# How the head stacks of block 2's attention are made: loads from DRAM, or one-hot products on chip

## The chip, the cores and the metric

The kernel runs on one core of a Trainium2 chip. The core's engines work side by side, each through its own instructions in order: TensorE (PE; its weight loads are listed apart as PEld) multiplies matrices into the accumulators (PSUM), VectorE (DVE) and ScalarE (ACT) work on elements, GpSimd (POOL) helps with elementwise work and fills, and SyncE (SP) issues all DMAs of this kernel into one queue. Times are device microseconds of a whole execution. The kernel before took 1585.57 us as the median of three runs (1581.46 to 1586.45).

## What is computed

The program is a perceiver of four blocks. 256 tokens of width 256, for a batch of 2, attend to a context of 4096 tokens, then to themselves, then pass through a feed-forward with experts; each step is added to the tokens. The change is in the self-attention of block 2. It scores by distance: queries, keys and values are one projection `Q`.

```
Q = (x @ W_k.T).reshape(B, S, H, dk).transpose(0, 2, 1, 3)      # 16 heads of 16
sq_norm = jnp.sum(Q * Q, axis=-1, keepdims=True)
dot = jnp.einsum('bhsk,bhtk->bhst', Q, Q)
scores = -(sq_norm - 2.0 * dot + sq_norm.transpose(0, 1, 3, 2)) * inv_sqrt_dk
attn = jax.nn.softmax(scores, axis=-1)
context_q = jnp.einsum('bhst,bhtk->bhsk', attn, Q)
merged = jnp.einsum('hkd,hvd->hkv', Wq_h, Wv_h)                 # W_k and W_v by head
attn_out = jnp.einsum('bhsk,hkv->bhsv', context_q, merged) * inv_sqrt_dk
return attn_out.transpose(0, 2, 1, 3).reshape(B, S, D) @ W_o.T
```

All of it is in float32. The kernel computes a product of two float32 matrices as three products of a high and a low part of each (`split` makes the parts, `mm3` the products).

## The kernel before, in words

**Lanes.** `run` interleaves two lanes of work, whose tiles carry a letter in the profile: `a` holds self-attention and feed-forward (`af(n, b)` runs those of block n for batch b), `x` the cross attentions. While lane `x` runs the cross attention of block 2 for batch 1 (`xattn`), lane `a` does the self-attention and feed-forward of block 2 for batch 0, then the queries of block 3's cross attention (`x3_queries`). Block 3's cross attention (`l3_xattn`) is a generator. First it takes the maxima of the scores of some key tiles, its early max steps: a product on PE (L1369), a maximum over 512 or 1024 columns on DVE (L1373, L1375). Then it hands over for block 2's work on batch 1 (`af(2, 1)`), and then it runs its main loop: maxima, scores (L1396), exponentials (L1397), values (L573). Its key tiles `xk` and query tiles `xq` are filled by a memset (L1281) and by loads from DRAM (L1358).

**Order.** Nothing in the source fixes the order of the instructions of an engine. The framework schedules all engines from its own model of durations (`schedule_with_timeline_sim=True`). A change of one stage can therefore move others. DMAs go out in the order of SP's instructions, one queue for all.

**Block 2's attention before (`l2_attn`).** For one batch: normalise and transpose the tokens, project (`proj_t`), split into parts `qT`. One product contracts all 128 partitions: a head's 16 channels of keys, high, high and low, against queries, high, low and high, and 2 + 2 rows for the squared norms against ones. So each head needs a stack, in which its parts lie one below the other on the partitions. [...] So `stack_tile` zeroes four tiles of four heads (two of keys, two of queries) on POOL and loads their rows of ones from a filling in DRAM; `qT` is written to DRAM (`aa2q`, 512 KB); and for each of the four groups of four heads six loads of 64 KB (`stack`) and two of norms (`rows_from`) build the stacks. The norms are made by PE: the squares times a selection matrix (`sq`, L1184), split, written to DRAM (`aa2s`). Then the scores (`mh_scores`: L566, exponentials L567), the values (`mh_values`, L573), the normalisation by the sums (`mh_finish`), and two projections; the product of `W_k` and `W_v` by head is folded into `bd`.

**Block 3's way.** `l3_ffn_attn`, the attention of block 3's feed-forward, makes stacks on chip: `picks` builds a matrix of shifted identities once, and `pair_stacks` multiplies it with the parts of a projection (L1591), so that the sum of two products holds two heads, one in each half of the partitions, with their parts in place. Its tile of ones and zeros, `extra`, adds the rows of ones during the eviction from PSUM (L1595 to L1599). Its row of shifts goes through two transposes, a copy and a DMA from SBUF to SBUF (L1640, L1642, L518).

Of the kernel before, what the change touches and what calls it, by code (L numbers as in the profile page):

```python
# [18 lines left out]
F32 = mybir.dt.float32  # L19
# [9 lines left out]
P = 128  # L29
# [171 lines left out]
def _consts():  # L201
# [7 lines left out]

    half = np.arange(2)[None, :, None] * 8 + (p // HD)[:, None, None]  # L210
    sq = np.where(half == np.arange(HEADS)[None, None, :], -0.5, 0.0).astype(np.float32)
# [10 lines left out]
        ("extra", ((p % 64 >= 48) & (p % 64 < 50)).astype(np.float32)[:, None]),  # L222
# [4 lines left out]
        ("sq", sq.reshape(P, -1)),  # L227
# [62 lines left out]
class Lane:  # L290
# [237 lines left out]
    def stack_tile(self, pool, tag, n, ones=(), heads=GRP):  # L528


        x = self.t(pool, [P, heads, n], tag, F32R, bufs=1)
        self.nc.gpsimd.memset(x.bitcast(F32), 0.0)
        for at, k in ones:
            for j in range(0, heads, GRP):
                self.rows_from(x[:, j : j + GRP, :].rearrange("p j n -> p (j n)"), at, k, self.top.fill_d[:k, : GRP * n])
        return x

# [19 lines left out]

    def mh_scores(self, mp, keys, queries, scale, tie=lambda inst: None):


        nc = self.nc
        p = self.t(mp, [P, GRP, S], "p", bufs=self.p_bufs)
        for a in range(0, GRP, 2):
            ps = self.score()
            for j in range(2):
                tie(nc.tensor.matmul(ps[:, j, :], lhsT=keys(a + j), rhs=queries(a + j), start=True, stop=True))  # L566
            self.last_exp = nc.scalar.activation(p[:, a : a + 2, :], ps, AF.Exp, scale=scale)  # L567
        return p
# [64 lines left out]
class Perceiver:  # L633
# [51 lines left out]
    def xattn_mean(self, xp, n, b, queries):  # L685
# [77 lines left out]
        def exponents(i):  # L763
            u, q = divmod(i, 2)
            p, su = k.t(xp, [P, self.UN], "p", bufs=2), k.t(k.sm, [P, 1], f"su{q}", bufs=4)
# [329 lines left out]
    def along(self, fp, g):  # L1095
# [5 lines left out]
        row = k.t(fp, [8, S], "grow", bufs=1)  # L1101
# [59 lines left out]

    def l2_attn(self, b, x):
# [3 lines left out]
        with k.pool("a2", bufs=1) as ap:  # L1166
            xnT = k.transposed(k.layernorm(x, ap), ap, "xnT")
            sel = k.const(ap, "sq").rearrange("p (m h) -> p m h", m=2)
# [4 lines left out]
            ks = [k.stack_tile(ap, f"k{i}", S, [(k.ADD, 2)]) for i in range(2)]  # L1173
            qs = [k.stack_tile(ap, f"q{i}", S, [(k.ADD + 2, 2)]) for i in range(2)]
            qT = k.t2(ap, [P, 2, S], "qT")
            sq = k.t(ap, [P, 2, S], "o")
            ps = k.proj_t(wk, xnT, 0)
            nc.scalar.activation(sq, ps, AF.Square)
            k.split(qT, ps)
            q_d = k.dram([2, 2, P, S], f"a2q{b}")  # L1180
            k.to_dram(qT, q_d)
            ps = k.mm()
            for m in range(2):
                nc.tensor.matmul(ps[:HEADS, :S], lhsT=sel[:, m, :], rhs=sq[:, m, :], start=m == 0, stop=m == 1)  # L1184
            sqs = k.t2(ap, [HEADS, S], "sqs")
            k.split(sqs, ps[:HEADS, :S])
            sqd = k.dram([2, HEADS, S], f"a2s{b}")
            for i, part in enumerate((sqs.h, sqs.l)):
                nc.sync.dma_start(sqd[i], part.bitcast(F32))
# [3 lines left out]
            k.copy(v[:, :, :, :HD], k.proj(wk, xnT).rearrange("p t (h d) -> p t h d", d=HD))  # L1193
            bd = k.t(ap, [P, 2, P], "bd")
# [6 lines left out]
            bdp = k.t2(ap, [P, 2, P], "bdp")  # L1201
            k.split(bdp, bd)
            o = k.t(ap, [P, 2, D], "o")
            for g in range(4):
                k4, q4 = ks[g % 2], qs[g % 2]
                g4 = slice(GRP * g, GRP * g + GRP)
                k.stack(k4, q_d, g4, k.KEYS)
                k.stack(q4, q_d, g4, k.QUERIES)
                k.rows_from(q4, k.ADD, 2, sqd[:, g4, :])
                k.rows_from(k4, k.ADD + 2, 2, sqd[:, g4, :])  # L1210
                acc = k.mm()
                ps = [k.mh_scores(ap, lambda j: k4[:, j, t * P : (t + 1) * P], lambda j: q4[:, j, :], 0.5) for t in range(2)]
                for t in range(2):
                    k.mh_values(ps[t], lambda j: v[:, t, 4 * g + j, :], acc, t == 0, t == 1)
                k.mh_finish(g, acc, o)()
            oT = k.transposed(o, ap, "xnT")
            mT = k.t2(ap, [P, 2, S], "qT")
# [8 lines left out]
    def l2_ffn(self, b, x):  # L1226
# [4 lines left out]
        with k.pool("f2", bufs=2) as fp:  # L1231
            br = k.row("f2.br", fp)
            xf = k.t(fp, [P, 2, S], "xf", bufs=1)
            xnT = k.transposed(k.layernorm(x, fp), fp, "xnT", plain=xf)
# [64 lines left out]
    def masks(self):  # L1299

        k, nc = self.a, self.nc
        with k.pool("mask", bufs=1) as mp:
# [8 lines left out]
            fill = k.t(mp, [4, 2048], "fill")  # L1311
            nc.gpsimd.memset(fill, 1.0)
            nc.sync.dma_start(self.fill_d, fill)
# [253 lines left out]

    PICK, PICK_BLOCKS = {"kl": 0, "ql": 1, "kh": 9, "qh": 17}, 25

    def picks(self, k, pool):  # L1570


        nc = self.nc
        x = k.t(pool, [P, 4, self.PICK_BLOCKS, HD], "pick", F32R, bufs=1)
        nc.gpsimd.memset(x.bitcast(F32), 0.0)
        eye = self.eye.rearrange("p (i a d) -> p i a d", i=4, a=2)
        for at in (2, 9, 10, 17, 19):
            nc.vector.tensor_copy(x[:, :, at : at + 5 : 4, :], eye)
        return x.rearrange("p i a d -> p i (a d)")

    def pair_stacks(self, k, pick, dst, src, kind, extra=None):


        nc = self.nc
        for m in range(2):
            for i in range(0, 4, 2):
# [339 lines left out]
```

## Time and profile before

| | us |
|---|---|
| median of three runs (1581.46, 1585.57, 1586.45) | 1585.57 |
| the profiled execution | 1590.7 |
| its span, from the first to the last instruction | 1588.9 |
| PE busy | 1387.5 (87%) |
| DVE busy | 1106.4 (70%) |
| ACT busy | 891.8 (56%) |
| POOL busy | 534.7 (34%) |
| mean clock that was granted to PE | 0.916 of full |

The profiled execution is 5.1 us above the median, which is within what runs of the kernel differ by. Busy times are sums over a span with stages of different limits: which engine bounds the kernel must be read stage by stage. Two consecutive matmuls overlap, so a matmul's own duration (0.28 us for 256 columns) is longer than its share of a busy queue. Where the profile names what ended an idle time ("<-DMA ak<-aa2q"), it is the event that came last, here the load of the stack tile `ak` from the DRAM tile `aa2q`. Names carry the lane's letter in front (`aqT` is `qT` of lane a).

| block 2's self-attention | batch 0 | batch 1 |
|---|---|---|
| projection written to DRAM | 721.41 | 932.10 |
| squares times the selection matrix, on PE | 721.53 | 930.14 |
| first scores on PE | 731.7 | 942.21 |
| output added to the tokens (L1223) | 790.35 | 986.11 |

### The profile page before, as it was taken

The page shows a single profiled execution, that of the slowest core. Times are in us where ns is not written, and L with a number is a line of the kernel's source. Part 1 is how long each engine was busy: PE and PEld are TensorE (multiplying, and loading weights), DVE is VectorE, ACT ScalarE, POOL GpSimd, SP SyncE. Part 2 cuts the span into 40 slices and gives each one's busy share as a digit, 9 for nine tenths or more (in the row PEclk, how much of TensorE's full clock was granted, in tenths as well). Part 3 has the DMA queues.
Part 4 walks back from the last instruction along what each step waited for, and adds up shares of the span by engine and source line. Part 5 has one row for each costly group of instructions (what it writes and reads, how often), then busy time and mean ns, then how long its engine had stood idle before and what let it go on. Part 6 is the DMA issues. An engine that isn't in the chain of part 4 may idle for free.

```text
span 1588.9 us, 29546 instructions
## 1 busy us (share of the span) xinstructions
PE 1387.5 (87%) x11278; PEld 1126.0 (71%) x11278; DVE 1106.4 (70%) x1895; ACT 891.8 (56%) x1669; POOL 534.7 (34%) x395
## 2 busy tenths in 40 slices
PE   6899798978999998989973679979999999888498
PEld 6898688968899998988973245645555554774387
DVE  6999755455577787865663666759999980566764
ACT  5676455556866656745631016648888889233242
POOL 6655244444455454663354000120000000530441
PEclk9999899979999999999996558879999999996699
DMA  8753165564556575546454512456676741200471
GB/s 292 224 150 115 51 177 172 187 192 160 166 160 207 161 217 162 160 143 187 134 143 122 85 59 57 111 131 114 113 116 111 114 71 31 85 1 3 175 254 35
DMA packets 126628, 212.32 MB, mean 134 GB/s; under 512 B 14212, under 2 KB 90532, under 8 KB 122964
## 3 DMA queue, kind: packets, MB, share of 16 engines
q1 hardware_dynamic: 126488, 210.45, 48.7%
q8 instruction: 89, 1.46, 0.4%
q14 instruction: 51, 0.42, 0.1%
HBM read 181.72 MB, written 29.01 MB: 133 GB/s over the span
## 4 chain that ended last, share of the span: by engine, by line
PE 46%; DVE 16%; DMA 9%; ACT 4%; POOL 3%; issue 2%; SPq 1%; DVEq 0%; ACTq 0%; POOLq 0%
PE amm L405 9%; PE xacc L573 7%; DVE xpm L1375 6%; PE xmm L405 5%; PE xf L1369 5%; PE xs L405 4%; PE xpr L405 3%; DMA awr<-in_w 3%; PE amm L1396 2%; DMA xk<-akh_d 2%; PE xs L1396 2%; PE amm L1756 2%; PE xmm L777 1%; PE amm L573 1%; POOL aw L397 1%
## 5 line engine op out<-in xcount | busy, mean ns | idle before, releaser
L1375 DVE TENSOR_REDUCE xpm<-xf 128x2 f32<-128x1024 f32 x232 | 281.7, 1222 | 34.2 <-PE xf L1369 31.9
L397 POOL TENSOR_TENSOR aw<-awr,aw 128x1024 fp32r<-128x1024 f32 (+1 forms) x61 | 145.7, 2390 | 299.8 <-ACT aw L395 294.0
L1397 ACT ACTIVATE xp<-amm 128x512 f32<-128x512 f32 x299 | 170.1, 595 | 31.0 <-PE amm L1396 17.9
L395 ACT CAST aw<-awr 128x1024 fp32r<-128x1024 f32 (+1 forms) x114 | 115.5, 1016 | 116.0 <-DMA awr<-in_w 69.5
L405 PE MATMUL xmm<-xvx,xpT 128*128 128x256 f32 x1152 | 167.0, 291 | 4.5 <-DVE xpT L780 2.5
L573 PE MATMUL xacc<-xp,xv 128*17 128x256 f32 x2048 | 165.7, 397 | 0.9 <-DVE xot L591 0.9
L405 PE MATMUL xs<-xkx,xqkT 128*128 128x256 f32 x1152 | 164.0, 286 | 1.4 <-POOL xkx L727 0.6
L727 POOL TENSOR_TENSOR xvx<-xraw,xvx 128x512 fp32r<-128x512 f32 x96 | 131.6, 1387 | 82.9 <-ACT xvx L725 72.1
L405 PEld LDWEIGHTS xmm<-xvx,xpT 128*128 128x128 f32 x1152 | 147.7, 193 | 8.0 <-issue 3.7
L405 PEld LDWEIGHTS xs<-xkx,xqkT 128*128 128x128 f32 x1152 | 149.2, 193 | 3.5 <-POOL xkx L727 1.0
L1397 ACT ACTIVATE xp<-xs 128x512 f32<-128x512 f32 x213 | 123.5, 595 | 37.1 <-PE xs L1396 22.5
L1369 PE MATMUL xf<-xk,xq 49*128 49x512 f32 x464 | 125.4, 530 | 15.8 <-DVE xpm L1375 6.9
L1369 PEld LDWEIGHTS xf<-xk,xq 49*128 49x128 f32 x464 | 46.7, 195 | 114.4 <-issue 79.8
L399 DVE TENSOR_TENSOR aw<-awr,aw 128x1024 fp32r<-128x1024 f32 (+1 forms) x53 | 81.2, 1533 | 66.5 <-ACT aw L395 66.2
L405 PE MATMUL amm<-axnT,aw 128*128 128x256 f32 x648 | 101.1, 313 | 11.7 <-ACT axnT L395 6.9
L405 PEld LDWEIGHTS amm<-axnT,aw 128*128 128x128 f32 x648 | 92.3, 216 | 20.3 <-ACT axnT L395 9.7
L405 PE MATMUL amm<-ah,aw 128*128 128x256 f32 x768 | 99.3, 285 | 6.6 <-ACT au L1002 3.3
L1396 PE MATMUL amm<-xq,xk 51*128 51x256 f32 x598 | 99.6, 297 | 4.2 <-DVE aqT L393 2.9
L727 POOL TENSOR_TENSOR xkx<-xraw,xkx 128x512 fp32r<-128x512 f32 x48 | 72.3, 1506 | 89.8 <-ACT xkx L725 89.7
L405 PEld LDWEIGHTS amm<-ah,aw 128*128 128x128 f32 x768 | 94.3, 191 | 9.3 <-ACT au L1002 3.9
L1420 POOL TENSOR_TENSOR ax<-ax,ax 128x128 f32<-128x128 f32 x8 | 3.7, 458 | 281.8 <-DVE ax L603 281.8
L1396 PEld LDWEIGHTS amm<-xq,xk 51*128 51x128 f32 x598 | 83.9, 188 | 18.2 <-issue 12.6
(545 smaller groups left out, 2918.0 us busy)
## 6 DMA issues: line engine op xcount, KB each, us to landing
awr<-in_w SPq DMA_DIRECT2D x106, 512.0 KB
xraw<-in_ctxT SPq DMA_DIRECT2D x108, 256.0 KB
xraw<-in_ctx SPq DMA_DIRECT2D x96, 256.0 KB
xk<-akh_d SPq DMA_DIRECT2D x128, 128.0 KB
av_d<-xkvv SPq DMA_DIRECT2D x16, 544.0 KB
xv<-av_d SPq DMA_DIRECT2D x32, 272.0 KB
akh_d<-xkvk SPq DMA_DIRECT2D x32, 256.0 KB
akl_d<-xkvk SPq DMA_DIRECT2D x32, 256.0 KB
```

Source lines behind the costliest of these rows:

```text
L395: nc.scalar.copy(dst.h, src)
L397: lo.tensor_tensor(dst.l, src, dst.h.bitcast(F32), ALU.subtract)
L399: nc.vector.tensor_sub(dst.l, src, dst.h)
L405: tie(self.nc.tensor.matmul(out, lhsT=x, rhs=y, start=start and i == 0, stop=stop and i == 2))
L573: inst = self.nc.tensor.matmul(acc[STRIP * j : STRIP * j + v(j).shape[1], :S], lhsT=v(j), rhs=p[:, j, :], start=start, stop=stop)
L727: nc.gpsimd.tensor_tensor(x.l, r, x.h.bitcast(F32), ALU.subtract)
L777: tie(nc.tensor.transpose(pst[:, t * P : (t + 1) * P], p[:, t * P : (t + 1) * P], self.eye))
L1369: tie(nc.tensor.matmul(ps[h], lhsT=q4[rows, j, t * P : (t + 1) * P], rhs=k4[rows, j, :], start=True, stop=True))
L1375: nc.vector.tensor_reduce(at, both.rearrange("p (h n) -> p h n", h=2), axis=AX.X, op=ALU.max)
L1396: tie(nc.tensor.matmul(ps[h][:, j, :], lhsT=ks[c][rows, a + j, s * P : (s + 1) * P], rhs=q4[rows, a + j, :], start=True, stop=True))
L1397: exps = [nc.scalar.activation(p[:, h, a : a + 2, :], ps[h], AF.Exp, scale=0.25) for h in range(2)]
L1756: nc.tensor.matmul(ps[:, f, :], lhsT=w1[half][:, c, f * P : (f + 1) * P], rhs=buf[:, c, e * cap : (e + 1) * cap], start=c == 0, stop=c == 1)
```

## The change

Block 2's attention makes its stacks on chip, as block 3's does, for all 16 heads at once: 32 one-hot products and 8 evictions per batch, four of keys and four of queries. Two heads share a stack, in the lower and the upper 64 partitions, of which 52 rows are used. The one-hot matrix is built once ahead of block 2 and stays. `stack_tile`, the filling in DRAM, the write of `qT` and the loads of stacks are gone. The squared norms now come from the projection for the values, whose tokens lie on the partitions: Square on ACT, a sum over 16 columns on DVE, and a new function `pair_rows` that splits them, transposes them, copies the rows and sends them by eight DMAs into the stacks' norm rows. Block 3's attention uses `pair_rows` too. Tiles share places to make room: the layer normalisation uses the tile of `o` (or `u` in the feed-forward), `bd` that of `o`, `bdp` that of `qT`, the feed-forward's row of gates that of `xf`, and `xattn` keeps three buffers of row sums for four.

```diff
-        ("extra", ((p % 64 >= 48) & (p % 64 < 50)).astype(np.float32)[:, None]),
+        ("extra", np.stack([(p % 64 >= at) & (p % 64 < at + 2) for at in (3 * HD, 3 * HD + 2)], axis=1).astype(np.float32)),
...
-        ("sq", sq.reshape(P, -1)),
...
-            p, su = k.t(xp, [P, self.UN], "p", bufs=2), k.t(k.sm, [P, 1], f"su{q}", bufs=4)
+            p, su = k.t(xp, [P, self.UN], "p", bufs=2), k.t(k.sm, [P, 1], f"su{q}", bufs=3)
...
-        row = k.t(fp, [8, S], "grow", bufs=1)
+        row = k.t(fp, [8, S], "xf", bufs=1)
...
+    PICK, PICK_BLOCKS = {"kl": 0, "ql": 1, "kh": 9, "qh": 17}, 25
+    def picks(self, k, pool):
+        nc = self.nc
+        x = k.t(pool, [P, 4, self.PICK_BLOCKS, HD], "pick", F32R, bufs=1)
+        nc.gpsimd.memset(x.bitcast(F32), 0.0)
+        eye = self.eye.rearrange("p (i a d) -> p i a d", i=4, a=2)
+        for at in (2, 9, 10, 17, 19):
+            nc.vector.tensor_copy(x[:, :, at : at + 5 : 4, :], eye)
+        return x.rearrange("p i a d -> p i (a d)")
+    def pair_rows(self, k, pool, x, scale, dsts):
+        nc, n = self.nc, x.shape[3]
+        parts = k.t(pool, [P, 2, 2, 2, n], "pr_both", F32R, bufs=1)
+        nc.vector.tensor_scalar(parts[:, :, :, 0, :], x, scale, None, ALU.mult)
+        for t in range(2):
+            nc.vector.scalar_tensor_tensor(parts[:, t, :, 1, :], x[:, t], scale, parts[:, t, :, 0, :].bitcast(F32), ALU.mult, ALU.subtract)
+        ps = k.mm()
+        for t in range(2):
+            nc.tensor.transpose(ps[: 4 * n, t * P : (t + 1) * P], parts.bitcast(F32)[:, t].rearrange("p h a j -> p (h a j)"), self.eye)
+        rows = k.t(pool, [4 * n, S], "pr_row", F32R, bufs=1)
+        nc.vector.tensor_copy(rows, ps[: 4 * n, :S])
+        for dst, at in dsts:
+            for h in range(2):
+                k.rows_from(dst, h * self.HALF + at, 2, rows[2 * n * h : 2 * n * (h + 1)])
+    def pair_stacks(self, k, dst, src, kind, extra=None):
+        nc, pick = self.nc, self.pick
+        for m in range(2):
+            for i in range(0, 4, 2):
+                ps = k.mm2()
+                for j in range(2):
+                    for n, part in enumerate((src.h, src.l)):
+                        at = self.PICK[kind + "hl"[n]] * HD
+                        nc.tensor.matmul(ps[:, j, :], lhsT=pick[:, i + j, at : at + P], rhs=part[:, m, :], start=n == 0, stop=n == 1)
+                to = dst[:, 4 * m + i : 4 * m + i + 2, :]
+                k.flip ^= 1
+                if extra is None:
+                    nc.vector.tensor_copy(to, ps) if k.flip else nc.scalar.copy(to, ps)
+                elif k.flip:
+                    nc.vector.tensor_scalar(to, ps, extra, None, ALU.add)
+                else:
+                    nc.scalar.activation(to, ps, AF.Identity, bias=extra)
     def l2_attn(self, b, x):
         k, nc = self.a, self.nc
         wk, wv = k.weights("a2.wk", "a2.wv")
         (wo,) = k.weights("a2.wo")
         with k.pool("a2", bufs=1) as ap:
-            xnT = k.transposed(k.layernorm(x, ap), ap, "xnT")
-            sel = k.const(ap, "sq").rearrange("p (m h) -> p m h", m=2)
+            xnT = k.transposed(k.layernorm(x, ap, "o"), ap, "xnT")
             diag = k.const(ap, "diag")
             k.mh_tiles(ap)
-            ks = [k.stack_tile(ap, f"k{i}", S, [(k.ADD, 2)]) for i in range(2)]
-            qs = [k.stack_tile(ap, f"q{i}", S, [(k.ADD + 2, 2)]) for i in range(2)]
+            ks, qs = (k.t(ap, [P, HEADS // 2, S], tag, F32R) for tag in "kq")
             qT = k.t2(ap, [P, 2, S], "qT")
-            sq = k.t(ap, [P, 2, S], "o")
-            ps = k.proj_t(wk, xnT, 0)
-            nc.scalar.activation(sq, ps, AF.Square)
-            k.split(qT, ps)
-            q_d = k.dram([2, 2, P, S], f"a2q{b}")
-            k.to_dram(qT, q_d)
-            ps = k.mm()
-            for m in range(2):
-                nc.tensor.matmul(ps[:HEADS, :S], lhsT=sel[:, m, :], rhs=sq[:, m, :], start=m == 0, stop=m == 1)
-            sqs = k.t2(ap, [HEADS, S], "sqs")
-            k.split(sqs, ps[:HEADS, :S])
-            sqd = k.dram([2, HEADS, S], f"a2s{b}")
-            for i, part in enumerate((sqs.h, sqs.l)):
-                nc.sync.dma_start(sqd[i], part.bitcast(F32))
+            k.split(qT, k.proj_t(wk, xnT, 0))
+            for dst, kind in ((ks, "k"), (qs, "q")):
+                self.pair_stacks(k, dst, qT, kind, self.extra[:, kind == "q" :][:, :1])
             v = k.t(ap, [P, 2, HEADS, STRIP], "v")
             nc.gpsimd.memset(v, 0.0)
             nc.gpsimd.memset(v[:, :, :, HD], 1.0)
-            k.copy(v[:, :, :, :HD], k.proj(wk, xnT).rearrange("p t (h d) -> p t h d", d=HD))
-            bd = k.t(ap, [P, 2, P], "bd")
+            ps = k.proj(wk, xnT)
+            k.copy(v[:, :, :, :HD], ps.rearrange("p t (h d) -> p t h d", d=HD))
+            sq = k.t(ap, [P, 2, D], "o")
+            nc.scalar.activation(sq, ps, AF.Square)
+            sums = k.t(k.sm, [P, 2, HEADS], "sq_sum")
+            nc.vector.reduce_sum(sums, sq.rearrange("p t (h d) -> p t h d", d=HD), axis=AX.X)
+            self.pair_rows(k, ap, sums.rearrange("p t (a h) -> p t h a", h=2), -0.5, [(ks, k.ADD + 2), (qs, k.ADD)])
+            bd = k.t(ap, [P, 2, P], "o")
             ps = k.mm2()
             for c in range(2):
                 for d in range(2):
                     k.mm3(ps[:, c, :], wk[d][:, c * P : (c + 1) * P], wv[d], d == 0, d == 1)
             for c in range(2):
                 nc.vector.scalar_tensor_tensor(bd[:, c, :], ps[:, c, c * P : (c + 1) * P], 0.25, diag, ALU.mult, ALU.mult)
-            bdp = k.t2(ap, [P, 2, P], "bdp")
+            bdp = k.t2(ap, [P, 2, P], "qT")
             k.split(bdp, bd)
             o = k.t(ap, [P, 2, D], "o")
             for g in range(4):
-                k4, q4 = ks[g % 2], qs[g % 2]
-                g4 = slice(GRP * g, GRP * g + GRP)
-                k.stack(k4, q_d, g4, k.KEYS)
-                k.stack(q4, q_d, g4, k.QUERIES)
-                k.rows_from(q4, k.ADD, 2, sqd[:, g4, :])
-                k.rows_from(k4, k.ADD + 2, 2, sqd[:, g4, :])
-                acc = k.mm()
-                ps = [k.mh_scores(ap, lambda j: k4[:, j, t * P : (t + 1) * P], lambda j: q4[:, j, :], 0.5) for t in range(2)]
+                acc, ps = k.mm(), []
+                for t in range(2):
+                    p = k.t(ap, [P, 2, 2, S], "p", bufs=k.p_bufs)
+                    for h in range(2):
+                        r = slice(h * self.HALF, h * self.HALF + k.ADD + 4)
+                        both = k.score()
+                        for j in range(2):
+                            nc.tensor.matmul(both[:, j, :], lhsT=ks[r, 2 * g + j, t * P : (t + 1) * P], rhs=qs[r, 2 * g + j, :], start=True, stop=True)
+                        nc.scalar.activation(p[:, :, h, :], both, AF.Exp, scale=0.5)
+                    ps.append(p.rearrange("p a h n -> p (a h) n"))
                 for t in range(2):
                     k.mh_values(ps[t], lambda j: v[:, t, 4 * g + j, :], acc, t == 0, t == 1)
                 k.mh_finish(g, acc, o)()
             oT = k.transposed(o, ap, "xnT")
-            mT = k.t2(ap, [P, 2, S], "qT")
+            mT = k.t2(ap, [P, 2, S], "k")
             ps = k.mm2()
             for c in range(2):
                 k.mm3(ps[:, c, :], bdp[:, c, :], oT[:, c, :], True, True)
...
-            xnT = k.transposed(k.layernorm(x, fp), fp, "xnT", plain=xf)
+            xnT = k.transposed(k.layernorm(x, fp, "u", bufs=2), fp, "xnT", plain=xf)
...
-            fill = k.t(mp, [4, 2048], "fill")
-            nc.gpsimd.memset(fill, 1.0)
-            nc.sync.dma_start(self.fill_d, fill)
...
-                parts = k.t(k.sm, [P, 2, 2, 2, 4], "sh_both8", F32R)
-                nc.vector.tensor_copy(parts[:, :, :, 0, :], nm)
-                nc.vector.tensor_sub(parts[:, :, :, 1, :], nm, parts[:, :, :, 0, :].bitcast(F32))
-                ps = k.mm()
-                for t in range(2):
-                    nc.tensor.transpose(ps[:16, t * P : (t + 1) * P], parts.bitcast(F32)[:, t].rearrange("p h a j -> p (h a j)"), self.eye)
-                sh = k.t(ap, [16, S], "sh_row", F32R, bufs=2)
-                nc.vector.tensor_copy(sh, ps[:16, :S])
-                for h in range(2):
-                    k.rows_from(qs[:, at : at + 4, :], h * self.HALF + k.ADD, 2, sh[8 * h : 8 * h + 8])
+                self.pair_rows(k, ap, nm, 1.0, [(qs[:, at : at + 4, :], k.ADD)])
...
+        self.extra = a.const(self.fix, "extra")
...
+                            else:
+                                self.pick = self.picks(a, early.enter_context(a.pool("pick")))
```

More of the change, by code (lines that the diff above doesn't have):

```diff
@@ L208, in _consts @@
     first = np.broadcast_to(8.0 - np.arange(8, dtype=np.float32), (P, 8))
-    half = np.arange(2)[None, :, None] * 8 + (p // HD)[:, None, None]
-    sq = np.where(half == np.arange(HEADS)[None, None, :], -0.5, 0.0).astype(np.float32)
     freq = (1.0 / np.float32(10000.0) ** (np.arange(0, 64, 2, dtype=np.float32) / np.float32(64))).astype(np.float32)
@@ L526 @@
     KEYS, QUERIES = (0, 0, 1), (0, 1, 0)
[L528 to L536, printed above, removed]
     def shift_rows(self, mp, nm, qs, step=1):
@@ L556, in shift_rows @@
         return rest
[L558 to L568, printed above, removed]
     def mh_values(self, p, v, acc, start, stop, after=None, tie=lambda inst: None):
@@ L1565, in f3_tiles, with l3_ffn_attn @@
         return qs, ks, v
[L1568 to L1586, printed above, removed]
-                ps = k.mm2()
-                for j in range(2):
-                    for n, part in enumerate((src.h, src.l)):
-                        at = self.PICK[kind + "hl"[n]] * HD
-                        nc.tensor.matmul(ps[:, j, :], lhsT=pick[:, i + j, at : at + P], rhs=part[:, m, :], start=n == 0, stop=n == 1)
-                to = dst[:, 4 * m + i : 4 * m + i + 2, :]
-                k.flip ^= 1
-                if extra is None:
-                    nc.vector.tensor_copy(to, ps) if k.flip else nc.scalar.copy(to, ps)
-                elif k.flip:
-                    nc.vector.tensor_scalar(to, ps, extra, None, ALU.add)
-                else:
-                    nc.scalar.activation(to, ps, AF.Identity, bias=extra)
-    def l3_ffn_attn(self, k, b, x, w, rows, tiles, picks, out):
+    def l3_ffn_attn(self, k, b, x, w, rows, tiles, out):
         nc = self.nc
@@ L1611, in l3_ffn_attn @@
             hT = k.transposed(hn, ap, "hT", scale="f3.g1", bias="f3.c1")
-            pick, extra = picks
-            for w, bias, dst, kind, add in ((wq, "f3.bq", qs, "q", None), (wk, "f3.bk", ks, "k", extra)):
-                self.pair_stacks(k, pick, dst, k.proj_t_split(w, hT, ap, "p", bias=bias, bufs=k.p_bufs), kind, add)
+            for w, bias, dst, kind, add in ((wq, "f3.bq", qs, "q", None), (wk, "f3.bk", ks, "k", self.extra[:, :1])):
+                self.pair_stacks(k, dst, k.proj_t_split(w, hT, ap, "p", bias=bias, bufs=k.p_bufs), kind, add)
             ps = k.proj(wv, hT)
@@ L1820, in run @@
         self.md = a.dram([B, L], "md")
-        self.fill_d = a.dram([4, 2048], "fill_d")
         blocks = (), (self.l1_attn, self.l1_ffn), (self.l2_attn, self.l2_ffn)
@@ L1891, in run @@
                 rows = [a.row(f"f3.{r}", x.wp) for r in ("bv", "bo", "g2", "c2")]
-                picks = self.picks(a, x.wp), a.const(x.wp, "extra")
+                self.pick = self.picks(a, x.wp)
                 x.mm_tags, x.score_tags, x.wraw, x.p_bufs = ["mm"], [(x, "mm")], a.wraw, 2
@@ L1901, in run @@
                         at = slice(2 * b, 2 * b + 2)
-                        self.l3_ffn_attn(k, b, xb[b], w, rows, self.f3_tiles(k, tp), picks, (base[:, at, :], h2[:, at, :], lg[:, at, :]))
+                        self.l3_ffn_attn(k, b, xb[b], w, rows, self.f3_tiles(k, tp), (base[:, at, :], h2[:, at, :], lg[:, at, :]))
         with self.psum(a, mm=6, acc=2), a.pool("wraw", bufs=4) as a.wraw, a.pool("w", bufs=7) as a.wp, a.pool("f3m", bufs=1) as pool:
```

## Prediction

> **What bounds the kernel now.** I read the page first (span, slices, the chain), then busy time by stretches around block 2, then the chain of waits there, then timelines and single tiles. The slices show TensorE (PE) busy nearly everywhere; its granted clock sags in slices 23 to 26. The stretches (us of the span; length; busy time and count of PE, PEld, DVE, ACT, POOL; granted clock; DMA share; GB/s):
>
> ```profile
> 713.00:740.00 27.00, 27.00 (x223) 25.00 (x221) 15.85 (x35) 15.92 (x36) 11.99 (x12) 1.00 0.64 199
> 790.00:809.00 19.00, 16.66 (x136) 15.65 (x135) 16.17 (x57) 9.00 (x20) 3.22 (x3) 1.00 0.09 29
> 900.00:930.00 30.00, 25.40 (x59) 12.35 (x57) 26.03 (x40) 1.09 (x3) 0.00 (x0) 0.50 0.02 4
> 930.00:945.00 15.00, 10.77 (x46) 7.21 (x44) 8.87 (x11) 4.54 (x10) 0.00 (x0) 0.73 0.31 93
> 945.00:970.00 25.00, 23.98 (x142) 12.37 (x142) 12.40 (x16) 10.86 (x21) 0.00 (x0) 0.57 0.18 55
> 970.00:1000.00 30.00, 28.00 (x240) 16.61 (x236) 21.06 (x33) 18.80 (x35) 3.06 (x2) 0.84 0.49 91
> 1040.00:1060.00 20.00, 11.12 (x70) 7.85 (x68) 10.45 (x15) 7.36 (x11) 5.45 (x3) 0.80 0.60 119
> 1100.00:1200.00 100.00, 97.35 (x1084) 51.83 (x1082) 96.42 (x98) 82.79 (x153) 3.45 (x7) 1.00 0.70 116
> ```
>
> There are four regimes. A, 713 to 809: block 2's attention of batch 0 beside cross attention, on a PE that is never idle until 790. B, 809 to 924: loads of keys and weights, then max steps. C, 924 to 1060: the attention of batch 1 beside the l3 loop, on a PE at a low clock. D, from 1060: a loop that VectorE (DVE) fills. The edit acts in A and C. The chain of waits through B and C (start, length, what):
>
> ```profile
> 808.70 0.70 DVE ax L834
> 811.05 3.52 POOL xk L1281 x2
> 827.13 7.29 DMA xk<-akh_d
> ...
> 932.10 4.68 DMA aa2q<-aqT
> 940.13 2.04 DMA ak<-aa2q
> 942.21 0.71 PE amm L566 x4
> ...
> 1045.86 5.28 DMA xk<-akl_d
> ```
>
> The way through DRAM stands in the chain for batch 1 only: write, stack load, first scores, 10.1 us from 932.10 to 942.21. For batch 0 PE had second-lane work meanwhile. Prices for the new steps come from block 3's attention, which already makes stacks with one-hot products, and from the memsets that go:
>
> ```profile
> L1591 PE MATMUL amm<-ap,apick x32: 276/281/390, 1414.4 to 1427.8; 128*128 128x256 f32 x32
> L1597 DVE TENSOR_SCALAR ak<-amm,ac_extra x2: 742/746/750, 1424.1 to 1426.5; 128x512 fp32r<-128x512 f32 x2
> L1599 ACT ACTIVATE ak<-amm,ac_extra x2: 688/690/691, 1426.0 to 1428.1; 128x512 fp32r<-128x512 f32 x2
> L518 SPq DMA_DIRECT2D aq<-ash_row x4: 610/614/631, 1441.4 to 1451.9; - x4
> L532 POOL MEMSET ak<- x4: 952/956/1092, 712.3 to 851.0; 128x1024 f32 x4
> ```
>
> **The change part by part.** A matmul's own duration (281 ns) overlaps its neighbours; what it adds to a full queue is the spacing: 12 in 1.44 us of the chain at full clock, 0.12 each, and 12 in 2.93 us at 932.68, 0.244 each, at half.
>
> *Before block 2 (375 to 440).* The changed order, listed without running it, holds 4 more ACT table loads beside block 1's feed-forward: 4 x 1.283 = 5.1 us of ACT, in a stretch where PE is 83 to 93% busy. 0 (PE covers it) to +5; nearer the first, +1. The new one-time tile for the products (a memset, five copies) and the dropped filling lie far ahead of use on POOL and DVE: 0, under PE's work; uncovered, some 5 us.
>
> *A.* Added on PE: 32 x 0.12 = 3.8, and two transposes, 0.2; removed: four products of squares, 0.97 (721.53). Net +3.1. Eight evictions (4 x 0.746 on DVE, 4 x 0.690 on ACT), Square and a sum (0.6 each) find DVE and ACT 60% busy; 0, covered by the second lane's products. The 39 DMA issues of a batch (fillings, writes, rows, stacks) leave SP's queue, where raw loads are mixed in; PE waited for none of them here, so no gain. Tiles that now share a place, and the second lane's row sums in three buffers for four, wait on steps that lie well ahead in the listing: 0, or one exponential (0.697) if one does not. The rows now come by eight DMAs after a sum over the v projection: rows' copy 0.40, eight issues of 0.614 = 4.9, landing about 2 (the stack load's 2.04): 7.3 us from the transposes to the first scores. In the new order 49 matmuls, 5.9 us, lie between: PE idles 1.4. SP's waiting for raw loads ahead of them would add more (one wait there is 4.6 long), and everything queued behind the rows, raw loads too, moves by it. The transposes of the feed-forward's input, which stood before those of cross attention's last output, now stand between them, 0.4 of PE on the chain that they were beside. So 3.1 + 1.4 = +4.5, by which cross attention, which releases B at 808.70, ends later. From below: 790 to 809 has 2.3 idle PE time, leaving +0.8; from above 4.5 + 4.6 = +9. I take +4. The output projection, after 72 more second-lane matmuls (8.6 us) than before, brings the feed-forward's gates later by about 8, but they stood ahead of waits for weights (awr lands at 840.05).
>
> A rule of the Trainium skill ("TensorE: Matmul & The Clock Gate", Part 3: Packing small matmuls) speaks for the change: products in separate row groups of the array run at once. The scores now contract 52 rows in halves at partitions 0 and 64. In block 3 the same form takes 0.43 us for four (1429.41 to 1429.84), 0.11 each, as 128 rows do. By the rule A would be up to 32 x 0.06 = 1.9 shorter; by the row nothing.
>
> *B.* Four memsets of 0.95, 850.09 to 853.7, stand on POOL just ahead of the normalisation (its step starts at 854.73) that feeds the queries, and then the loads up to 894.78. They go: up to -3.7. But the 6.95 us of "issue" in front of it hold weight casts too, and keys' loads at 1.0 share of DMA set the pace again at 874. On SP the second load of gate weights moves behind five more key loads of 128 KB, 3.2 at the 205 GB/s of this stretch. Between -4 and +3; -1, the middle, rounded to the chain's side (the next memsets, 866.67, wait for these queries).
>
> *C.* PE takes 32 more products at half clock, 7.8, and two transposes, 0.5, less the squares, 1.89 (930.14): +6.4. Their evictions share DVE with max steps of 1.23 each that come every 2.5 us: a slip of one, +1.2. Then a new wait in the removed one's place. Gone: PE idle 1.32 + 2.70 = 4.0 ahead of 942.21. New, after the v projection: Square 0.6, sum 0.65, three small steps 0.5, a max step between 1.2, transposes 0.6, rows 0.4, issues 4.9, landing 2.0: 10.9. Against it PE has the folded product (1.85) and three pairs of max products (2.4): idle 6.6. Behind the waiting scores, in PE's one queue, stand the l3 loop's products, and DVE waits for those. So 6.4 + 1.2 + 6.6 - 4.0 = +10. D passes it on: it is DVE-bound at 96%, its work and order are the same from there. From above, with one more SP wait as in A, +15. From below, the clock: PE's 62.8 busy us from 930 to 1000 at .73, .57, .84 would be 45.0 at full clock, 17.7 less: 10 - 17.7 = -8, less what the products themselves lose at full clock (3.9): -12. I take +10, the nearest rows being 900 to 930, PE 85% busy at 0.50, and 945 to 970, 96% busy at 0.57.
>
> Those rows can be set against the same page of the skill, Part 1, by which about 3.4 us of sustained work release the full clock. By the rule 14 products would be slow and 18 fast, 5.6 for 7.8, and C +8; the rows differ from it, and by them it is +10.
>
> *Block 3's own feed-forward and attention (E)*: one more small DVE step per call, 4 x 0.17 = 0.7, and rows with one buffer for two; 0 to +1.5, +0.5.
>
> Sum: 1 + 4 - 1 + 10 + 0.5 = +14.5. The profiled execution took 1590.7 (span 1588.9 and 1.8 around it): 1605.2 after. It stands 5.1 above the median of the runs shown, 1585.57, so the median becomes 1600.1: 1600.
>
> **Rivals.**
> *A larger loss: the row DMAs stall.* SP is one queue in order, and stack rows come last before use; for it, the 4.6 us wait there; against, PE has 49 products to spend. Both batches hit: A +9, C +15: 14.5 + 5 + 5 = +24.5, 1610.
> *Same: a later stall takes it up.* From 1040 to 1060 PE is idle 8.9 of 20 us behind loads of keys and weights (1045.86). If these keep their time while C moves, 14.5 - 8.9 = +5.6, and with A's lower bound (0.8 for 4) +2.4: 1588. Against: the loads are issued from 1043.38 on, when PE's earlier reads free the buffers, so they move along.
> *Faster: the clock.* No wait at 942 and a dense run of products: the clock goes to full from there. C = -12: 1 + 4 - 1 - 12 + 0.5 = -7.5: 1578. It decides from a saving by the clock of 19.3 of the 21.6 us above (17.7 + 3.9): then the sum is below -4.8. For it: 970 to 990 did run at full clock; against: 945 to 970.
> *The change does not do what it says.* 16 DMAs of rows stay, and scores still wait for DMA. That is in the sum; were nothing to reach the chain, 1586, which I count under same.
>
> **How the numbers follow.** Forecast 0.57, larger loss 0.15, same 0.13, faster 0.15. No change that a measurement of this kernel can tell is about 0.3%, 4.8 us: 1580.8 to 1590.3. The forecast's own range is 1592 to 1608 (C from +5 to +15, A from +1 to +9, not all at once), nearly all of it slower. Slower 0.57 + 0.15 = 0.72. Range for 8 in 10: up to the larger loss with some beyond, 1614; down into the faster case, 1579, leaving its lower half and little above.
>
> **What would show it.** PE between the stack products and the first scores of batch 1 idle by 5 or more, ended by a DMA of rows; first scores there 10 to 17 us after where they were, measured from the max steps' end (924.18), and the feed-forward's end later by some 10. Cross attention's end +4 against 808.70. The loop from 1100 unchanged in length. The prediction is wrong if the granted clock from 930 to 1000 rises clearly, if PE finds other products to fill the wait, or if the time is lost or won outside A and C.

## The result, and the profile after

| | before | after |
|---|---|---|
| median, five runs each (us) | 1585.57 (1579.5 to 1588.3) | 1593.6 (1590.67 to 1596.89) |
| ratio, 95% interval | 1 | 1.0056 [1.0031, 1.0081] |
| profiled execution, its span | 1590.7, 1588.9 | 1590.67, 1588.9 |

The change costs 8.9 us by the ratio (0.0056 of 1585.57; 4.9 to 12.8). The forecast was +14.5. The two profiled spans are equal all the same: before's profiled execution lies 5.1 above its median, after's 2.9 below. By the clock records PE stood at half clock for 267 us of before's span and for 236 us of after's. So these two traces can't be subtracted as wholes; they have to be read stage by stage, and with more traces than two.

The stretches of the changed kernel, with the columns and windows shown for before, but for 790 to 809:

```profile
713.00:740.00 27.00, 26.70 (x224) 26.18 (x223) 20.98 (x44) 16.45 (x34) 8.79 (x11) 1.00 0.46 138
900.00:930.00 30.00, 24.78 (x52) 11.26 (x52) 27.79 (x42) 0.59 (x1) 0.00 (x0) 0.50 0.06 18
930.00:945.00 15.00, 14.71 (x61) 11.55 (x61) 8.60 (x11) 3.33 (x5) 0.00 (x0) 0.56 0.01 2
945.00:970.00 25.00, 18.96 (x139) 11.64 (x137) 16.46 (x23) 12.93 (x24) 0.00 (x0) 0.80 0.08 25
970.00:1000.00 30.00, 27.72 (x281) 15.42 (x280) 22.37 (x30) 20.97 (x40) 1.57 (x1) 1.00 0.40 73
1040.00:1060.00 20.00, 12.35 (x80) 9.95 (x78) 7.70 (x15) 5.83 (x8) 6.95 (x4) 0.83 0.44 148
1100.00:1200.00 100.00, 97.57 (x1082) 51.95 (x1080) 96.70 (x95) 82.69 (x153) 2.10 (x5) 1.00 0.69 116
```

PE still has next to no gap from 713 to 790 (0.3 us in the first row) and still stands at half clock from 900 to 930. From 945 to 1000 it has clocks of 0.80 and 1.00, where before's profile had 0.57 and 0.84. The chain of waits of the changed kernel:

```profile
817.18 0.69 DVE ax L809
...
826.40 5.88 DMA xk<-akh_d
...
954.71 2.19 DMA aq<-apr_row
957.03 1.21 PE amm L1232 x3
...
1047.99 5.16 issue
```

The way through DRAM has left the chain, and a DMA of norm rows stands in its place, ahead of the first scores of batch 1.

For the stages I take fixed points that every kernel here has: the end of the cross attention of block 2 for batch 0 (start ends, A begins), that for batch 1 (A ends, B begins), the first, third and eighth maximum rows of block 3's loop (B, C, D end), and the last instruction. The same view with these points as its windows, before:

```profile
692.30:809.40 117.10, 111.60 (x909) 102.58 (x909) 73.99 (x193) 64.17 (x139) 38.87 (x37) 0.99 0.48 142
809.40:924.86 115.46, 66.22 (x259) 45.26 (x258) 63.75 (x96) 14.95 (x22) 37.87 (x31) 0.62 0.53 116
924.86:1094.07 169.21, 151.35 (x1179) 92.56 (x1181) 115.15 (x156) 92.17 (x163) 19.30 (x13) 0.80 0.43 98
```

and after:

```profile
695.03:817.87 122.84, 115.49 (x931) 104.87 (x930) 80.39 (x194) 67.35 (x141) 36.36 (x33) 0.99 0.38 116
817.87:928.45 110.58, 66.68 (x265) 45.66 (x266) 64.62 (x108) 15.31 (x23) 32.67 (x27) 0.62 0.52 121
928.45:1097.85 169.40, 147.35 (x1209) 93.54 (x1211) 119.30 (x164) 93.58 (x166) 19.99 (x13) 0.86 0.37 85
```

The second column is the stage's length. A is 5.7 longer, B 4.9 shorter, C the same; the start is 2.7 longer (692.30 to 695.03).

### The profile page after: what moved, and what is told of

It is laid out like the page before. It is cut to its first block, busy times and chain, and to the rows that moved or that the text cites. A ratio compares the mean times of both kernels' runs of the same rounds, so it can differ in the third digit from the quotient of the medians.

```text
span 1588.9 us, 29569 instructions
## 1 busy us (share of the span) xinstructions
PE 1383.3 (87%) x11338; PEld 1126.6 (71%) x11338; DVE 1119.6 (70%) x1920; ACT 902.6 (57%) x1679; POOL 527.3 (33%) x387
## 4 chain that ended last, share of the span: by engine, by line
PE 44%; DVE 19%; DMA 6%; ACT 5%; issue 3%; POOL 3%; SPq 1%; DVEq 0%; ACTq 0%; POOLq 0%
PE amm L402 8%; DVE xpm L1394 8%; PE xacc L548 6%; PE xmm L402 5%; PE xs L402 4%; PE xf L1388 4%; PE xpr L402 3%; PE amm L1415 2%; DMA awr<-in_w 2%; DMA xk<-akh_d 2%; PE amm L1731 2%; PE xs L1415 1%; PE xmm L752 1%; POOL aw L394 1%; DVE xpm L1392 1%
## 5 line engine op out<-in xcount | busy, mean ns | idle before, releaser
L1416 ACT ACTIVATE xp<-amm 128x512 f32<-128x512 f32 x299 | 170.1, 595 | 31.4 <-PE amm L1415 16.0
L402 PE MATMUL amm<-axnT,aw 128*128 128x256 f32 x648 | 105.9, 321 | 15.0 <-ACT axnT L392 6.9
L402 PEld LDWEIGHTS amm<-axnT,aw 128*128 128x128 f32 x648 | 96.7, 225 | 24.2 <-ACT axnT L392 9.5
```

Source lines behind the costliest of these rows:

```text
L402: tie(self.nc.tensor.matmul(out, lhsT=x, rhs=y, start=start and i == 0, stop=stop and i == 2))
L1416: exps = [nc.scalar.activation(p[:, h, a : a + 2, :], ps[h], AF.Exp, scale=0.25) for h in range(2)]
```

## The experiments

All stages of all traces, in us, from the same points; "loads" counts ACT's table loads:

| kernel | ratio to before, interval | loads | start | A | B | C | D | E |
|---|---|---|---|---|---|---|---|---|
| before | 1 | 17 | 692.3 | 117.1 | 115.5 | 169.2 | 208.9 | 286.0 |
| after | 1.0056 [1.0031, 1.0081] | 21 | 695.0 | 122.8 | 110.6 | 169.4 | 208.7 | 282.4 |
| 1 batch 0 alone | 1.0100 [1.0054, 1.0146] | 21 | 706.2 | 122.9 | 115.2 | 164.9 | 208.9 | 284.4 |
| 2 batch 1 alone | 1.0083 [1.0047, 1.0119] | 21 | 696.1 | 117.1 | 111.6 | 170.1 | 208.9 | 285.7 |
| 3 norms first | 1.0079 [1.0049, 1.0110] | 21 | 699.3 | 124.1 | 109.6 | 174.7 | 208.7 | 283.0 |
| 4 no row DMAs | 1.0059 [1.0027, 1.0091] | 21 | 693.4 | 123.3 | 111.1 | 165.6 | 208.6 | 282.9 |
| 5 before, constant early | 1.0045 [1.0011, 1.0080] | 21 | 700.9 | 117.5 | 113.0 | 166.4 | 208.7 | 283.7 |
| 6 after, constant late | 1.0028 [1.0001, 1.0055] | 17 | 691.3 | 122.8 | 109.4 | 169.0 | 208.6 | 285.3 |
| 7 batch 1 alone, late | 0.9989 [0.9958, 1.0020] | 17 | 691.7 | 116.6 | 110.5 | 174.4 | 208.9 | 285.8 |
| 8 before, 52 rows | 0.9991 [0.9964, 1.0017] | 17 | 698.2 | 123.7 | 112.3 | 163.7 | 208.7 | 283.8 |
| 9 products twice, late | one run | 17 | 689.0 | 126.0 | 111.9 | 169.0 | 208.6 | 282.7 |
| 10 no query stacks, late | one run | 17 | 693.1 | 121.0 | 110.5 | 166.8 | 208.6 | 286.3 |
| 11 before, 52 rows in batch 1 | 0.9948 [0.9918, 0.9977] | 17 | 691.3 | 116.6 | 110.8 | 161.1 | 208.6 | 284.8 |
| 12 after, other early spot | 1.0016 [0.9986, 1.0046] | 17 | 687.2 | 122.6 | 111.6 | 180.9 | 208.9 | 278.0 |

Single executions spread: before's ran from 1568.5 to 1602.3 over all comparisons. A and D repeat within 1 us or less where a kernel has the same work there, the start and C do not; they go with the time at half clock (C holds 40 to 82 us of it). Ratios are over 5 to 12 runs of a kernel and 5 to 26 of before; runs 9 and 10 have one execution each and no ratio.

**1 and 2. One batch by products, the other through DRAM.**

```diff
+    def l2_attn(self, b, x):
+        return self.l2_attn_new(b, x) if b == 0 else self.l2_attn_old(b, x)     # 2: b == 1
```

> The stacks of batch 0 by one-hot products, those of batch 1 by the way through DRAM as before. In the two profiles at hand batch 0's cross attention ends 8.5 us later (809.40 to 817.87), of which 2.7 were there before block 2 and 5.7 come in stretch A, and B gives back 4.9. Theory 'C' (the loss lies with batch 1, as my prediction had it, +10 of +14.5): 1586 to 1589, ratio to before 1.000 to 1.002. Theory 'A and the stretch before it' (C costs nothing in the end): 1592 to 1594, ratio 1.004 to 1.006, with first scores of batch 1 about 10 us after the max steps' end, as before.

> The mirror image: batch 0 through DRAM as before, batch 1 by one-hot products. Theory 'C': 1592 to 1595, ratio 1.004 to 1.006. Theory 'A and the stretch before it': 1585 to 1588, ratio 0.999 to 1.002. Both: the first scores of batch 1 some 11 us later against the max steps' end than before, and if C costs nothing in the end, the maximum rows that follow (third of eight) stand at most 2 us later against that same point.

Measured: 1.0100 and 1.0083. Neither theory holds: each half comes out no cheaper than the whole (the intervals overlap), so much of the cost is likely something that both halves share. The stages split cleanly nevertheless. A is long (122.9) only where batch 0 has the products, and B is short (111.6) only where batch 1 has them. Both starts are late: 706.2 and 696.1.

**3 and 4. The wait for the rows.** The first moves the value projection and the norms, all but the DMAs, ahead of the stack products; the second leaves the eight DMAs out.

```diff
             k.split(qT, k.proj_t(wk, xnT, 0))
+            # v, Square, reduce_sum and pair_rows up to the row copy stand here
             for dst, kind in ((ks, "k"), (qs, "q")):
                 self.pair_stacks(...)
+            send()                                   # 3: the eight row DMAs
...
-            self.pair_rows(k, ap, sums..., -0.5, [(ks, k.ADD + 2), (qs, k.ADD)])
+            self.pair_rows(k, ap, sums..., -0.5, [])  # 4
```

> The changed kernel with the value projection, the squares, their sums, transposes and the row copy ahead of the stack products; only the row DMAs remain behind them. Theory 'the wait for the rows' (PE idle in front of the first scores of batch 1): their first scores come 4 to 6 us earlier against the max steps' end, and the time falls by 2 to 5 against the changed kernel: 1589 to 1592. Theory 'the added products' (32 per batch, PE's own time): the first scores come earlier but the time stays within 1.5 of 1593.6.

> The changed kernel without the eight row DMAs of a batch: the norms are summed, split and transposed but not sent, and the exponent's scale is 0.001 for 0.5, so that it stays finite; every other instruction is there. Theory 'the wait for the rows': first scores follow the transposes at once in both batches, 4 to 7 us earlier in batch 1, and the time is 1587 to 1590. Theory 'the added products': 1592 to 1594.

The first scores of batch 1 do come earlier: 24.5 us after the first maximum row in both, against 28.6 in the changed kernel (17.4 before). The time does not follow: 1.0079 and 1.0059, for the changed kernel's 1.0056. So the wait for the rows is there, but no price of it shows: a gain of 2 to 5 us, as the theory of the wait had it, lies outside the interval of run 3 (from 1.0049, the changed kernel's own interval left aside), though not outside that of run 4 (from 1.0027). In A, removing the DMAs changes nothing either (123.3).

**5, 6 and 12. The constant.** The kernels with a late start all have 21 table loads. Lists of the instructions showed why: the load of `extra`, a DMA of 128 x 2 numbers, is now issued at the start, and with it alone the framework's schedule takes another order up to block 2. So one run puts that load alone into the kernel before, one takes it out of the start of the changed kernel, and one leaves it at the start but at another spot.

```diff
         self.first = a.const(self.fix, "first")
+        self.extra = a.const(self.fix, "extra")      # 5: this alone, in the kernel before
...
-        self.extra = a.const(self.fix, "extra")      # 6: away from the start of the changed kernel
-                                self.pick = self.picks(a, early.enter_context(a.pool("pick")))
+                                pool = early.enter_context(a.pool("pick"))
+                                self.pick = self.picks(a, pool)
+                                self.extra = a.const(pool, "extra")
...
         self.eye = a.const(self.fix, "eye")
+        self.extra = a.const(self.fix, "extra")      # 12: here, ahead of the tokens' loads
```

> The kernel before with one thing of the change: the constant of ones and zeros, now of two columns, is loaded at the start for the whole run (one small DMA) and not in block 3. Block 2's attention is the old one. The listing shows that this alone gives the order of the changed kernel up to block 2, with 21 ACT table loads for 17. Theory 'the new order ahead of block 2 costs': ratio 1.004 to 1.008 (1591 to 1598), cross attention of block 0 for batch 0 ends near 120 against 117.7, and the stretch from there to 692 is 3 to 8 longer. Theory 'block 2 itself': 1584 to 1587, ratio 0.999 to 1.002.

> The changed kernel with that constant loaded only ahead of block 2 (and again in block 3); the listing shows the order of before up to block 2, with 17 table loads. Theory 'the new order ahead of block 2 costs': the time falls by 6 or more against the changed kernel, ratio to before 0.998 to 1.003 (1582 to 1590), A 123 and B 110.6 long as in the changed kernel. Theory 'block 2 itself': 1592 to 1596, ratio 1.004 to 1.007.

> The changed kernel with the constant loaded at the start too, but right behind the identity and ahead of the tokens; the listing shows 17 ACT table loads and nearly the order of before up to block 2. Theory 'the new order ahead of block 2 costs 6 to 7': ratio 1.001 to 1.004 as with the late constant (1588 to 1592), cross attention of block 2 for batch 0 ends at 692 to 694. Theory 'an early DMA costs it, whatever the order': ratio 1.005 or more, and 696 or later.

Measured: 1.0045 for the load alone, with block 2 untouched; 1.0028 for the changed kernel without it; 1.0016 with it at the other spot, where 17 table loads remain. The first interval lies above 1. The second is 4.4 us under the changed kernel, where 6 or more was expected. The third speaks against "an early DMA costs it, whatever the order" by its start (687.2, earlier than either theory had it) and its ratio, though the ratio's interval reaches to 1.0046. ACT's table loads between 360 and 450 us, by groups (count, busy us, mean ns, idle before), in before:

```profile
L1002 ACT ACT_TABLE_LOAD x6 | 7.7, 1283 | 0.6 <-PE amm L405 0.5
L766 ACT ACT_TABLE_LOAD x6 | 7.7, 1283 | 0.1
```

and in run 5:

```profile
L1002 ACT ACT_TABLE_LOAD x8 | 10.3, 1283 | 1.5 <-PE amm L405 1.4
L766 ACT ACT_TABLE_LOAD x6 | 7.7, 1283 | 0.1
L771 ACT ACT_TABLE_LOAD x2 | 2.6, 1283 | 0.0
```

Two kinds of function alternate more often on ACT (L1002 of block 0's feed-forward with L766 and L771 of the cross attention). The start ends at 698.5 on average over the six traces with 21 loads, at 691.8 over the eight with 17: 6.7 apart, with single traces from 693 to 706 and from 687 to 698. The loads themselves (4 x 1.283 = 5.1 of ACT) are not the whole of it: the stretch that holds them, from about 350 us to the end of the third cross attention near 500, is 3.6 longer on average, the one from the end of the second cross attention (196) to there 3.3, with no load added; 1.4 stand ahead of it, and 1.6 are won back behind. The six traces also stand longer at half clock in the start, 53.8 us for 47.5, which is worth up to 3.2; whether the new order brings that was not separated.

**7. Batch 1 alone, with the late constant.** The edits of 2 and 6 together.

> As the kernel with one-hot stacks for batch 1 alone, and the constant loaded late. A is 117.1 long as before, B 111.6 (3.9 less than before, the memsets of batch 1's stacks being gone from POOL), C within 3 of before. Theory 'order ahead of block 2': ratio 0.995 to 1.000, 1577 to 1585, faster than before by up to 5. Theory 'block 2 itself, in C': 1590 or more.

Measured 0.9989. A is 116.6 and B 110.5, as expected; C, 174.4, is not within 3 of before in this trace, and a gain is not shown. Runs 2 and 7 differ by the constant's place alone, and by 14.9 us: with 7.1 (run 5 against before) and 4.4 (the changed kernel against run 6) that makes three pairs of one sign, whose size is not resolved. In the largest the mean granted clock differs too, 0.919 and 0.924.

**9 and 10. Does PE have room in A?**

```diff
-                for j in range(2):
+                for j in [0, 1] * twice:              # 9: twice = 2 for batch 0
...
+            if b == 0:
+                qs = ks                               # 10
-            for dst, kind in ((ks, "k"), (qs, "q")):
+            for dst, kind in ((ks, "k"), (qs, "q"))[: 1 + b]:
```

> The kernel with the late constant, with batch 0's 32 one-hot products issued twice over (64, same evictions). Theory 'PE has no room in A': A grows by 32 x 0.12 = 3.8, from 122.8 to 126.6, and B gives back less than 1 of it. Theory 'A's 5.7 are mostly waits for evictions and the order': A 123 to 124.5, since the second pass fills the waits.

> The kernel with the late constant, leaving out batch 0's query stacks: 16 products and 4 evictions less, its scores taken from the key stacks on both sides (and the exponent's scale 0.001 there). Theory 'PE has no room in A': A shrinks by 16 x 0.12 = 1.9, to 121. Theory 'waits for evictions': it shrinks by 3 or more, to 119.5 or less.

A is 126.0 with 32 products more than the 122.8 of run 6 and 121.0 with 16 fewer: 3.2/32 = 0.10 and 1.8/16 = 0.11 us each. The second keeps only half the evictions and shrinks by no more than its products. So PE has no room in A, and the evictions are covered.

**8 and 11. The memsets.** A contraction of only the 52 rows that hold data needs no zeroed tile, with the way through DRAM left as it was.

```diff
-        self.nc.gpsimd.memset(x.bitcast(F32), 0.0)   # in stack_tile; 11: kept for b == 0
...
-                ps = [k.mh_scores(ap, lambda j: k4[:, j, ...], lambda j: q4[:, j, :], 0.5) for t in range(2)]
+                r = slice(0, k.ADD + 4)              # 11: slice(0, P if b == 0 else k.ADD + 4)
+                ps = [k.mh_scores(ap, lambda j: k4[r, j, ...], lambda j: q4[r, j, :], 0.5) for t in range(2)]
```

> The kernel before, with one thing: scores contract the 52 rows that hold data, so that the stack tiles need no memset (eight of 0.95 us on POOL go, four of them ahead of the normalisation that feeds block 3's queries). The way through DRAM stays. Theory 'B's gain is those memsets': A 117 long, B 110 to 112 against 115.5, C 165 to 169 as before, ratio 0.995 to 0.999 (1577 to 1584). Theory 'B's gain comes from the absent DMAs or another order': B 115 and ratio 1.

> The kernel before, with batch 1's stack tiles alone left without memsets (its scores contract 52 rows); batch 0 as before. Theory 'B's gain is the four memsets ahead of the normalisation, and 52-row scores between 128-row products cost PE time only in A': A 117 long, B 111 to 113 against 115.5, C 164 to 169, ratio 0.996 to 0.999 (1580 to 1585). Theory 'nothing to gain there': ratio 1.000 or more with B at 115.

POOL's timeline in front of the normalisation that feeds block 3's queries, in before:

```profile
850.09 1.85 POOL L532 MEMSET ak<- 128x1024 f32 x2
851.88 1.85 POOL L532 MEMSET aq<- 128x1024 f32 x2
853.66 0.96 POOL L1191 MEMSET av<- 128x1024 f32 x1
854.73 1.51 POOL L409 TENSOR_TENSOR abn_rs<-abn_ve,amhalf 128x2 f32<-128x2 f32 x2
```

and in run 11:

```profile
847.27 0.95 POOL L1192 MEMSET av<- 128x1024 f32 x1
848.28 0.15 POOL L1193 MEMSET av<- 128x32 f32 x1
848.79 1.50 POOL L409 TENSOR_TENSOR abn_rs<-abn_ve,amhalf 128x2 f32<-128x2 f32 x2 [0.37 <-DVE abn_ve L424]
```

Before, the normalisation's step waits for POOL to finish its memsets; without them it waits 0.37 for DVE. DVE was held as well: the step in front of it, which takes 0.29 in run 11, ended in before only 0.03 us behind POOL's last memset of 128x1024:

```profile
851.37 3.28 DVE L424 TENSOR_SCALAR abn_ve<-abn_mv 128x2 f32<-128x2 f32 x2
```

B is 112.3 in run 8 and 110.8 in run 11, with every DMA of the old way in place: B's gain is the memsets. Run 8 as a whole shows no gain: in its trace A grows (123.7, of which its 7.0 us at half clock make up to 3.5), and the start ends late (698.2). Run 11 keeps A and is faster than both kernels: 1575.6 median in 12 runs, 0.9948 [0.9918, 0.9977]. B explains 4.7 of its 8.2 (3.7 by the averages below); C was 161.1 in its trace, with 55 us at half clock for before's 69, and whether that is more than the clock's luck stays open.

Why 52 rows cost PE time in A is seen in PE's timeline of the changed kernel (start, modelled length, line, tile, shapes, count):

```profile
747.54 0.50 PE L1232 MATMUL amm<-aq,ak 52*128 52x256 f32 x2
747.97 0.62 PE L402 MATMUL xs<-xkx,xqkT 128*128 128x256 f32 x3
748.52 0.51 PE L1232 MATMUL amm<-aq,ak 52*128 52x256 f32 x4
748.95 1.70 PE L402 MATMUL xpr<-xkx,xw 128*128 128x256 f32 x12
```

against before:

```profile
735.79 0.40 PE L566 MATMUL amm<-aq,ak 128*128 128x256 f32 x2
736.03 0.52 PE L405 MATMUL xmm<-xvx,xpT 128*128 128x256 f32 x3
```

Read the distance to the next start. Two scores of 128 rows take 0.24. Two of 52 rows between products of 128 rows take 0.43, and four of 52 rows, two in each half of the partitions, also take 0.43. In the records the two halves start 6 ns apart. At a change between 128 and 52 rows, either way, two spacings are longer than 0.12: 0.21 up to the first product of the new kind, whose weight load starts together with it (747.54) and not 0.12 ahead as between products of 128 rows, and 0.22 behind it. So the halves do run at once, as the Trainium skill states ("TensorE: Matmul & The Clock Gate", Part 3: Packing small matmuls); and each change of the number of rows costs 0.19. A of the changed kernel has nine groups of 52-row products, with 15 such changes (three groups end at products of 128 rows and 32 columns, where before shows the same 0.21); they cost 2.8, and the halves win back 1.6.

## Why the prediction was right or wrong

The direction and the range held: 1593.6 in 1579 to 1614. The sum, 14.5 for a measured 8.9, rests on terms of which one was far too small and one far too large: the start by 5.7, C by 5.4. That they nearly cancel is luck.

- **Before block 2 (forecast +1, 0 to +5): wrong, too small.** Run 5 prices it at 1.0045, +7.1 (1.7 to 12.7), run 6 at 4.4; the starts say 6.7, clock included. The step saw the four table loads (beside block 0's feed-forward, not block 1's) and let PE cover them, in a stretch where PE was 83 to 93% busy; that stretch alone is 3.6 longer, and the stretches ahead of it, which it left out, 4.7. It didn't ask what had made the order change: the load of one constant, which costs about half of the loss or more and has nothing to do with how the stacks are made.
- **A (+4, +0.8 to +9): right in kind, short in size.** Four traces with batch 0 as in the change give 122.6 to 122.9, five with the old way and 128 rows 116.6 to 117.5: +5.8. Added products bound it, as said (runs 9 and 10). By the counts there are 22 more in A (x909 to x931), at most 2.6; changes of row count, 1.2 net; PE idle, 1.1 more; half clock, 1.0 (2.1 us more of it): up to 5.9 in all. The waiting of 1.4 for the rows was not it (run 4). The comparison of rule and row went wrong: "0.43 us for four" was read as 0.11 each, so no gain from the halves. It was the halves' gain of 0.23 and 0.19 for changes of row count in one number.
- **B (-1, -4 to +3): right in kind, too cautious.** 110.9 on average in the eleven traces where those memsets are gone, 114.6 in the three others: -3.7, just the four memsets. The second gate load that was moved behind five key loads cost nothing that shows.
- **C (+10, -12 to +15): the delay of the scores was right, its price wrong.** The first scores stand 28.6 after the first maximum row for 17.4: +11.2, in the 10 to 17 named. PE idles 5.7 between the stack products and them, as the prediction's sign had it (5 or more), but in four gaps, of which only the last ends with the DMA of rows and the others with max steps on DVE:

```profile
957.03 1.21 PE L1232 MATMUL amm<-aq,ak 52*128 52x256 f32 x3 [1.60 <-DMA aq<-apr_row]
```

  The same stretch to the third maximum row is 171.4 on average over the seven traces with products and norms as in the change, 166.8 over the three with 128 rows and DRAM: +4.6. (They hold 56.0 and 60.1 us at half clock on average; with half of that taken off as an estimate, +6.6.) The step that failed is "behind the waiting scores, in PE's one queue, stand the l3 loop's products". They do not all stand behind. The groups of maxima on DVE from the first maximum row to the end of the attention, 924.86 to 986.10 in before and 928.45 to 997.30 in after:

```profile
L1375 DVE TENSOR_REDUCE xpm<-xf 128x2 f32<-128x1024 f32 x21 | 25.7, 1223 | 19.4 <-PE xf L1369 19.2
```

```profile
L1394 DVE TENSOR_REDUCE xpm<-xf 128x2 f32<-128x1024 f32 x27 | 33.0, 1223 | 11.9 <-PE xf L1388 9.5 <-PE xs L1415 1.7
```

  By the attention's end six more steps of the loop are done, five of them ahead of the first scores (9 for 4), and DVE's idle time falls from 19.4 to 11.9. This is not the clock of one trace: C holds 64 of these steps in every trace, and by the attention's end 26 to 28 of them are done wherever batch 1 has the products, 21 in the five traces where it has not. That work is missing later: from the attention's end to the third maximum row 99.9 us for 107.3. The prediction had named this as what would make it wrong ("if PE finds other products to fill the wait"). Runs 3 and 4 show it from the other side, where the scores come 4 us sooner, the attention ends only 1 us sooner, and no gain shows.
- **D: right; E: not to be told.** D is 208.6 to 208.9 everywhere. E, 282.4 to 286.3 but for one trace of 278.0, varies too much to show +0.5.
- **Rivals.** The faster one by the clock did not come. In the profiled pair the clock behind 945 did rise (0.80 and 1.00 for 0.57 and 0.84), which the prediction had named as a sign of being wrong; but the clock varies from run to run with either kernel, and C holds about as much half clock with the products as without (56.0 and 60.1 on average). The one by which a later stall takes the loss up came in part, by another way: loop steps, not the loads at 1045.
- **The sum.** With the traces' terms it is 6.7 + 5.8 - 3.7 + 4.6 = 13.4, just above the measured 4.9 to 12.8. Part of the gap can be the clock: within the executions of a kernel 0.01 of granted clock goes with about 11 us, and the five of the changed kernel have 0.923 on average, where before's in the other comparisons have 0.920, so an estimate of 3 us. The rest is not resolved. Block 2 alone, 6.7 by the traces, measures +4.4 (0.2 to 8.7) in run 6.

## What to carry to other kernels

Where a framework orders the instructions, a difference of order far ahead of the edit is a cost of its own: find the line that causes it, and put that line alone into the old kernel. A wait on the chain is only worth what the engine's queue cannot do meanwhile: count the steps of the other lane between two fixed points before pricing it. And before replacing data movement by products on an engine that is full, look for what else rode along with the old way; here it was a memset of rows that nobody needed, and removing that for one batch won 8.2 us where the whole change lost 8.9.

## What the runs showed of the hardware

- A change between products of 128 and of 52 rows costs PE 0.19 us, each way, in two spacings of 0.21 and 0.22 for 0.12; two 52-row products in the two halves of the partitions start 6 ns apart and run at once.
- While POOL's memsets ran in before, a DVE step on 128x2 numbers took 3.28 us for 0.29 and ended with them; what held it was not tested.
- PE's clock stands at half in stretches of 3.4, 6.8, 10.2, 17.1, 23.9 and 81.9 us, among them 861.2 to 943.1 of the changed kernel, where PE was 83% busy from 900 to 930. Where they fall differs between traces (in C, 40 to 82 us), and executions of one and the same kernel differ by up to 2%. The Trainium skill ("TensorE: Matmul & The Clock Gate", Part 1) has windows of about 3.4 us, after one of which sustained work releases the clock; the lengths fit that grain; the long stretch does not fit the release, if 83% busy counts as sustained.
- One DMA of 128 x 2 numbers, at the start, moved the end of the kernel before by 7.1 us (1.7 to 12.7); with it the framework gave everything behind it another order. At another early spot, which left the order nearly as it was, the start was not later (687.2).
